# The last image's convolution: one channel tile's taps on ScalarE and GpSimd, the other two tiles' sums in PSUM

## The chip, the cores and the metric

The kernel runs on one core of a Trainium2 chip. A core has five engines with queues of their own: TensorE (PE, matrix products, with its weight loads listed apart as PEld), VectorE (DVE), ScalarE (ACT), GpSimd (POOL) and SyncE (SP, which starts transfers). SBUF is the working memory; TensorE writes its products to PSUM, which is divided into banks of 512 float32 values for each of the 128 partitions. The metric is the device time of one execution in microseconds, lower is better.

## The reference

The input x has 8 images of 384 channels and 64x64 pixels, all float32. Two layers follow each other, each adding its result to its input:

```python
# layer 0: window attention (8x8 windows, half of the heads on a shifted grid)
x = x + attention(group_norm(x), ...)
# layer 1: what this change is about
t = einsum('bchw,oc->bohw', group_norm(x), w_in)
t = irfft2(rfft2(blocks_of_8x8(t)) * fft_filter)          # per channel
t = depthwise_conv_3x3(t, w_dw)                            # 9 taps per channel
x1, x2 = t[:, :192], t[:, 192:]
x = x + einsum('bchw,oc->bohw', gelu(x1) * x2, w_out)
```

The change touches the depthwise convolution, the product of gelu(x1) and x2, and the output product with w_out.

## The kernel before

An image is worked on in 8 strips of 8 rows (512 pixels). The 384 channels are three tiles of 128 partitions, so an operation on one tile of a strip is 128x512. The attention of one image and the second layer of the image before it run interleaved; when the attention of the last image (number 7) is over, only second layers are left: the last strips of image 6's and all of image 7's.

The second layer of a strip goes through these pieces:

- `normal_x1` (L652, ScalarE) normalises the strip into xn. `mix` (four products pt on TensorE, L662 copies to SBUF on ScalarE) applies w_in. `transform` (products pf, multiplied by the filter on VectorE at L679) goes to the frequency domain, and `back` (products pz) returns from it.
- `inner` and `borders` (L707, L716, L717, ScalarE) bring pz to SBUF as z, a tile of 10 rows of 66 pixels, and exchange one border row with the strip above.
- `conv` makes the nine taps. Tap 4 is a scaled copy on ScalarE (L752), the other eight are one operation on VectorE each (L758): z shifted, times the channel's weight in `dw_sb`, plus the sum so far in zz. Taps 6 to 8 need the lower border row, so they wait for the strip below.
- For the last image and for strip 7 of image 6, the table `on_pe` gives TensorE the first five taps of tile 1: `conv_taps` multiplies z by diagonal matrices (made by `tap_matrices`) and adds up in a PSUM tile pc, from which VectorE's taps 5 to 8 go on. For the very last strip TensorE makes five taps of tile 2 and all nine of tile 1.
- `gate` applies Gelu (L771, L772, ScalarE) and multiplies (L773, L774, L775, VectorE). Hidden channels are laid out so that tiles 0 and 1 hold x1 and x2 of 128 channels, and tile 2 holds both halves of the other 64.
- `finish` is the output product pw on TensorE, its addition to the strip's input on VectorE (L797, L799) and the transfer to HBM (L800).

Each call `at(place, piece, ...)` gives a piece a place on a common axis on which a strip takes two units. The pieces are issued in the order of these places. Matmuls keep that order on TensorE. On the other engines a scheduler may reorder what has no explicit order between it, and it then inserts the waits. PSUM is used in two ways: four single banks (`psum`) that are taken in turn, and two pairs of banks (`psum2`).

`FETCHES` and the counting before the last loop belong to empty instructions that are put among the matmuls of images before the last; the pieces that the change touches lie behind them.

The lines that the tables below and the text refer to are those of this listing:

Of the kernel before, what the change touches and what calls it, by code (L numbers as in the profile page):

```python
# [7 lines left out]
F32 = mybir.dt.float32  # L8
AF = mybir.ActivationFunctionType
# [3 lines left out]
P = 128  # L13
# [24 lines left out]
def block_kernel(ctx: ExitStack, tc: tile.TileContext, out, x, consts, fsel, wqk, wv, bqk, bv,  # L38
# [21 lines left out]
    def matmul(*args, **kw):  # L60
        tc.keep_in_program_order(nc.tensor.matmul(*args, **kw))  # L61
        fetched["count"] += 4

        n = min(fetched["empty"], fetched["share"])
        for _ in range(n):
            tc.keep_in_program_order(nc.tensor.nop(hint="empty"))
        fetched["empty"] -= n
        fetched["count"] += n
# [8 lines left out]
    def row512(tag, bufs, name):  # L77
        return sb.tile([P, ST], F32, tag=tag, bufs=bufs, name=name)
# [222 lines left out]
    def at(place, piece, *args):  # L301
        plan.append((place, len(plan), piece, args))
# [1 line left out]
    xs, ys, y2s, qks, vs, os_, ots, x1s, zs = ({} for _ in range(9))  # L304

    z_bufs = [cp.tile([P, WS + 2, SW + 2], F32, name=f"z{i}") for i in range(7)]
    zs["count"] = 0
    for z in z_bufs:
        nc.gpsimd.memset(z[:, :, 0:1], 0.0)
        nc.gpsimd.memset(z[:, :, SW + 1:SW + 2], 0.0)  # L310
# [408 lines left out]


    TAPS = (4, 0, 1, 2, 3, 5, 6, 7, 8)
    on_pe = {(B - 1, s): {1: 5} for s in range(NS - 1)}
    on_pe[B - 2, NS - 1] = {1: 5}
    on_pe[B - 1, NS - 1] = {2: 5, 1: 9}

    def tap_matrices():
        d = strip("y", 3, "taps").rearrange("p k (t c) -> p (k t) c", c=P)
# [6 lines left out]
    def conv_taps(b, s):  # L734
        pc = psum2(f"pc_{b}_{s}")
        for i, (m, n) in enumerate(on_pe[b, s].items()):
            zs[b, s, "zz", m] = pc[:, i]
            for j in range(n):
                dy, dx = TAPS[j] // 3, TAPS[j] % 3
                matmul(pc[:, i], zs["taps"][m][:, j], zs[b, s, m][:, dy:dy + 8, dx:dx + SW],  # L740
                       start=(j == 0), stop=(j == n - 1))

    def conv(b, s, m, tap):

        z = zs[b, s, m]
        n = on_pe.get((b, s), {}).get(m, 0)
        if tap < max(n, 1):
            return
        if tap == max(n, 1):
            zz = row512("zz", 5, f"zz_{b}_{s}_{m}")  # L750
            if n == 0:
                after_out(nc.scalar.activation(zz.rearrange("p (r c) -> p r c", c=SW), z[:, 1:9, 1:SW + 1],  # L752
                                               AF.Copy, scale=dw_sb[:, m, 4:5]))
                zs[b, s, "zz", m] = zz
            zs[b, s, "acc", m] = zz
        acc, old = zs[b, s, "acc", m], zs[b, s, "zz", m]
        dy, dx = TAPS[tap] // 3, TAPS[tap] % 3
        i = nc.vector.scalar_tensor_tensor(acc.rearrange("p (r c) -> p r c", c=SW),  # L758
                                           z[:, dy:dy + 8, dx:dx + SW], dw_sb[:, m, TAPS[tap]:TAPS[tap] + 1],
                                           old.rearrange("p (r c) -> p r c", c=SW), ALU.mult, ALU.add)  # L760

        if b < B - 1 and m and tap == 1:
            tc.keep_in_program_order(i)
        if b < B - 1:
            after_softmax(i)
        zs[b, s, "zz", m] = acc

    def gate(b, s):
        zz = {m: zs[b, s, "zz", m] for m in range(KC)}
        g1 = row512("g1", 2, f"g1_{b}_{s}")  # L770
        nc.scalar.activation(zz[0], zz[0], AF.Gelu)  # L771
        nc.scalar.activation(g1[64:P], zz[2][0:64], AF.Gelu)  # L772
        nc.vector.tensor_tensor(g1[0:64], g1[64:P], zz[2][64:P], ALU.mult)  # L773
        nc.vector.tensor_tensor(g1[64:P], g1[64:P], zz[2][64:P], ALU.mult)  # L774
        nc.vector.tensor_tensor(zz[0], zz[0], zz[1], ALU.mult)  # L775
        zs[b, s, "g"] = zz[0], g1

    def finish(b, s):


        g0, g1 = zs[b, s, "g"]
        t = xs[b, s, "finish"]

        pw = [psum(f"pw_{b}_{s}_{m}") for m in range(2)]
        pw2 = psum2(f"pw2_{b}_{s}")
        full, lo, hi = slice(0, ST), slice(0, 256), slice(256, ST)
        pw = [(pw[0], 0, full), (pw[1], 1, full), (pw2[:, 0, lo], 2, lo), (pw2[:, 1, lo], 2, hi)]

        for i, half, r in ((0, 0, 0), (1, 1, 1), (0, 1, 0), (1, 0, 1), (2, 0, 0), (3, 1, 1), (2, 1, 0), (3, 0, 1)):
            p, m, tok = pw[i]  # L790
            rows, cols = slice(r * 64, (r + 1) * 64), slice(half * 64, (half + 1) * 64)
            matmul(p[cols], wo_sb[rows, 1, m * P + half * 64:m * P + half * 64 + 64], g1[rows, tok],
                   start=True, stop=False)
        for p, m, tok in pw:
            matmul(p, wo_sb[:, 0, m * P:(m + 1) * P], g0[:, tok], start=False, stop=True)
        for m in range(2):
            nc.vector.tensor_tensor(t[:, m, :], pw[m][0], t[:, m, :], ALU.add)  # L797
        by_half = t[:, 2, :].rearrange("p (o n) -> p o n", o=2)
        zs["added"] = nc.vector.tensor_tensor(by_half, pw2[:, :, lo], by_half, ALU.add)  # L799
        nc.sync.dma_start(out=rows_of(out[b], s), in_=t)  # L800
# [5 lines left out]
    for b in range(B):  # L806
# [73 lines left out]
        for s in range(NS):  # L880
            u = first + 2 + 2 * s
            at(u - 0.84, load, b, s, "mix")
            at(u + 0.02, normal_x1, b, s)
            for i in range(4):
                at(u + (0.28, 0.45, 0.60, 0.78)[i], mix, b, s, i)
            for j in range(2):
                at(u + (0.995, 1.02)[j], transform, b, s, j)
            if b < B - 1:
                at(u + 1.985, small_tiles, u + 2)
            at(u + 1.99, back, b, s)  # L890
            at(u + 2.08 if b < B - 1 or s < NS - 1 else u + 1.991, borders, b, s)

            for n, m in enumerate((0, 2, 1)):
                for tap in range(1, 6):
                    at(u + (2.62, 3.10, 3.5)[n] + 0.05 * tap + (0.4 if n == 2 and tap > 3 else 0), conv, b, s, m, tap)
                for tap in range(6, 9):
                    at(u + 4.2 + 0.25 * (n * 3 + tap - 6) / 9, conv, b, s, m, tap)
            if (b, s) in on_pe:
                at(u + 2.3, conv_taps, b, s)
            at(u + 5.16, load, b, s, "finish")  # L900
            at(u + 4.5, gate, b, s)
            at(u + 6.10, finish, b, s)
# [6 lines left out]
    count, dense, empty = fetched["count"], [], [0] * len(order)  # L909
    for i, (piece, args) in enumerate(order):  # L910
        count += 4 * sum(on_pe[args].values()) if piece is conv_taps else FETCHES.get(piece.__name__, 0)
        if piece in (qk_tile, project):
# [121 lines left out]
```

## Time and profile before

| what | value |
| --- | --- |
| time, median of 3 runs | 3572.18 us (3568.28 to 3581.91) |
| profiled execution: span | 3571.7 us (the page gives no other time for it) |
| TensorE busy | 3489.3 us, 98% |
| VectorE busy | 3059.8 us, 86% |
| ScalarE busy | 2475.3 us, 69% |
| GpSimd busy | 953.0 us, 27% |
| L758, VectorE taps | 1483 + 9 operations, 744 ns in the middle |
| L752, ScalarE scaled copies | 182 operations, 719 ns |
| L380, GpSimd sums of 128x512 | 122 operations, 1282 ns in the middle, 1263 to 2361 |
| pc<-z,taps on TensorE | 108 matmul records, 47.8 us in all |

The span runs from the first instruction to the last. A busy share is an average over the whole span, so the stage that the change touches has to be looked up by itself. A float32 matmul appears as two records. In a row of instructions, "out<-in" are the program's names with the buffer numbers left out, then the shape, "x" the count, and a bracket gives the idle time before it and what ended it.

### The profile page before, as it was taken

The numbers are of one execution on the slowest core, as the hardware profiler recorded it, in microseconds if no ns is written. First come the engines' busy times: TensorE is split into PE (matmuls) and PEld (weight loads), VectorE is DVE, ScalarE is ACT, GpSimd is POOL, SyncE is SP. The second block draws the span as 40 slices with busy tenths as digits, with TensorE's granted clock in tenths as the row PEclk, the third lists the DMA queues.
The fourth block names the chain that finished last, engine by engine and source line by source line (L and its number), as shares of the span: only waits on it lengthen the run. The fifth ranks groups of instructions, "written<-read, shape, count | busy, mean of one in ns | idle before, by whom it ended". The sixth has DMA issues, their size and how long they took to land.

```text
span 3571.7 us, 93732 instructions
## 1 busy us (share of the span) xinstructions
PE 3489.3 (98%) x36598; PEld 2209.2 (62%) x36598; DVE 3059.8 (86%) x4370; ACT 2475.3 (69%) x3983; POOL 953.0 (27%) x1616
## 2 busy tenths in 40 slices
PE   7999999999999999999999999999999999999998
PEld 5666666666666666666666666666666656666554
DVE  4766689889988899888998889988899888887988
ACT  4777677768777677776777767777777768776442
POOL 5333222223222232222232223222232223221000
PEclk8999999999999999999999999999999999999999
DMA  4333333234333334333333334333334233333431
GB/s 124 115 124 111 104 113 133 101 105 158 127 121 116 114 125 158 103 112 134 126 130 124 118 106 143 133 103 134 123 120 148 100 106 122 100 104 108 156 116 72
DMA packets 177254, 427.45 MB, mean 120 GB/s; under 512 B 26784, under 2 KB 29371, under 8 KB 176840
## 3 DMA queue, kind: packets, MB, share of 16 engines
q1 hardware_dynamic: 139984, 370.54, 29.6%
q0 software_dynamic: 36416, 50.65, 5.1%
q8 instruction: 318, 5.21, 0.6%
q14 instruction: 96, 0.79, 0.1%
q10 hardware_dynamic: 440, 0.27, 0.0%
HBM read 270.21 MB, written 100.79 MB: 104 GB/s over the span
## 4 chain that ended last, share of the span: by engine, by line
PE 88%; DVE 8%; ACT 2%; DMA 1%; issue 1%; SPq 0%; ACTq 0%; DVEq 0%
PE pq L61 26%; PE pr L61 14%; PE pvv L61 13%; PE pt L61 11%; PE pw L61 6%; DVE zz L758 4%; PE pA L61 4%; PE pz L61 3%; PE pS L61 3%; PE pT L71 3%; PE pf L61 2%; PE ln L61 1%; DVE t L679 0%; DMA x_stats<-in_x_dram 0%; DVE e L535 0%
## 5 line engine op out<-in xcount | busy, mean ns | idle before, releaser
L758 DVE SCALAR_TENSOR_TENSOR zz<-z,dw_sb,zz 128x512 f32<-128x512 f32 x1483 | 1117.8, 783 | 26.2 <-ACT z L716 14.9
L61 PE MATMUL pq<-y,wqk_sb 128*128 128x512 f32 x2160 | 999.8, 600 | 0.9 <-DVE y L436 0.8
L613 POOL DMA_DIRECT2D oT<-o x960 | 480.4, 508 | 981.3 <-ACT z L716 442.4
L61 PEld LDWEIGHTS pq<-y,wqk_sb 128*128 128x128 f32 x2160 | 400.7, 190 | 459.9 <-issue 416.1
L61 PE MATMUL pt<-wi_sb,xn 128*128 128x384 f32 x1536 | 536.0, 487 | 7.6 <-ACT kcd L468 4.8
L61 PE MATMUL pr<-oT,wp_sb 128*128 128x512 f32 x1152 | 522.5, 592 | 0.0
L61 PE MATMUL pvv<-wv_sb,y 128*128 128x192 f32 x2880 | 508.5, 326 | 0.0
L61 PEld LDWEIGHTS pvv<-wv_sb,y 128*128 128x128 f32 x2880 | 470.7, 190 | 47.7 <-issue 32.7
L61 PEld LDWEIGHTS pt<-wi_sb,xn 128*128 128x128 f32 x1536 | 289.4, 190 | 234.9 <-issue 76.7
L450 POOL COPY y<-y 128x384 f32<-128x384 f32 x112 | 83.4, 744 | 1136.6 <-PE pvv L61 665.1
L61 PEld LDWEIGHTS pr<-oT,wp_sb 128*128 128x128 f32 x1152 | 218.6, 190 | 268.6 <-issue 249.9
L468 ACT ACTIVATE kcd<-pq,bqk_sb 32x512 f32<-32x512 f32 x512 | 348.4, 680 | 9.0
L468 ACT ACTIVATE qab<-pq,bq_sb,cst 96x512 f32<-96x512 f32 (+1 forms) x256 | 197.6, 772 | 199.2 <-PE pq L61 196.6
L501 ACT COPY v<-pvv 128x384 f32<-128x384 f32 x256 | 121.6, 475 | 212.6 <-PE pvv L61 211.4
L468 ACT ACTIVATE kab<-pq,bqk_sb 96x512 f32<-96x512 f32 (+1 forms) x256 | 174.1, 680 | 96.9 <-PE pq L61 92.4
L468 ACT ACTIVATE qcd<-pq,bq_sb,cst 96x512 f32<-96x512 f32 (+1 forms) x256 | 197.5, 772 | 35.9 <-PE pq L61 29.1
L662 ACT COPY t<-pt 128x384 f32<-128x384 f32 x256 | 122.5, 479 | 128.9 <-PE pt L61 124.8
L528 DVE TENSOR_TENSOR e<-pS,bias 128x512 f32<-128x512 f32 (+2 forms) x200 | 108.1, 547 | 114.6 <-PE pS L61 114.4
L380 POOL TENSOR_TENSOR sq<-sq 128x512 f32<-128x512 f32 x122 | 200.9, 1647 | 5.8
L535 DVE TENSOR_TENSOR e<-e,mx 128x1024 f32<-128x1024 f32 x128 | 198.7, 1553 | 4.1
L61 PE MATMUL pw<-zz,wo_sb 128*128 128x512 f32 (+1 forms) x512 | 183.4, 501 | 0.0
L545 DVE TENSOR_REDUCE rc<-e 128x16 f32<-128x1024 f32 x128 | 155.0, 1211 | 29.6 <-ACT e L540 29.6
(151 smaller groups left out, 5185.7 us busy)
## 6 DMA issues: line engine op xcount, KB each, us to landing
x_add<-in_x_dram SPq DMA_DIRECT2D x64, 768.0 KB, 9.6
x1d<-x_add SPq DMA_DIRECT2D x64, 768.0 KB, 3.7
x_mix<-x1d SPq DMA_DIRECT2D x64, 768.0 KB, 5.4
x_finish<-x1d SPq DMA_DIRECT2D x64, 768.0 KB, 7.2
out_dram<-x_finish SPq DMA_DIRECT2D x64, 768.0 KB, 4.2
x_norm<-in_x_dram SPq DMA_DIRECT2D x61, 768.0 KB, 7.4
x_stats<-in_x_dram SPq DMA_DIRECT2D x56, 768.0 KB, 7.6
oT<-o POOLq DMA_DIRECT2D x192, 96.0 KB, 3.8
```

Source lines behind the costliest of these rows:

```text
L61: tc.keep_in_program_order(nc.tensor.matmul(*args, **kw))
L71: tc.keep_in_program_order(nc.tensor.transpose(*args, **kw))
L380: nc.gpsimd.tensor_tensor(sq[:, 0, :], sq[:, 0, :], sq[:, k, :], ALU.add)
L450: nc.gpsimd.tensor_copy(dst[:, :, :, :, 0:4], src[:, :, :, :, 4:8])
L468: return nc.scalar.activation(dst[to:to + n], pq[of:of + n], AF.Identity, bias=bias[of:of + n], scale=scale)
L501: nc.scalar.copy(v[:, 384 * g:384 * (g + 1)], pvv[:, 0:384])
L528: nc.vector.tensor_tensor(e5[:, odd, :, a:z, :], pS[:, odd, :, a:z, :], bias_t[br, kind, odd].unsqueeze(2).to_broadcast([P, 2, z - a, 64]) ...
L535: zs["soft"] = nc.vector.tensor_tensor(e, e, mx.unsqueeze(2).to_broadcast([P, 2 * NS, 64]), ALU.subtract)
L545: nc.vector.tensor_reduce(rc, e, AX.X, ALU.add)
L613: nc.gpsimd.dma_start(out=oT[to % P:to % P + z - a, to // P, rows], in_=o[row + a:row + z, h // 2, of:of + n])
L662: nc.scalar.copy(t1, pt[:, 0:C])
L758: i = nc.vector.scalar_tensor_tensor(acc.rearrange("p (r c) -> p r c", c=SW), z[:, dy:dy + 8, dx:dx + SW], dw_sb[:, m, TAPS[tap]:TAPS[tap] ...
```

## The change

For strip 7 of image 6 and strips 0 to 6 of image 7 (the list `on_pool`), three things change.

1. Tile 1 leaves TensorE and VectorE. ScalarE makes all nine taps as scaled copies, two to a buffer (three buffers, taken over from the attention, whose tags are "o", "e" and "eT"), and GpSimd adds them up in SBUF (`pool_taps`).
2. Tiles 0 and 2 keep their sum in a pair of PSUM banks from tap 4 to the gate; VectorE's taps read and write it in place. Gelu of tile 0 writes its result to SBUF.
3. The product of tile 0 and tile 1 in `gate` moves from VectorE to GpSimd. As a PSUM pair is in use for the sums, `finish` takes three single banks for its output in place of two banks and a pair, and its third tile is computed as one 512-wide piece.

The last strip of image 7 keeps its taps on TensorE and VectorE.

```diff
-    on_pe = {(B - 1, s): {1: 5} for s in range(NS - 1)}
-    on_pe[B - 2, NS - 1] = {1: 5}
-    on_pe[B - 1, NS - 1] = {2: 5, 1: 9}
+    on_pe = {(B - 1, NS - 1): {2: 5, 1: 9}}
+    on_pool = [(B - 2, NS - 1)] + [(B - 1, s) for s in range(NS - 1)]
...
+    def pool_taps(b, s, taps):
+
+        z = zs[b, s, 1]
+        for j in range(0, len(taps), 2):
+            tag = ("o", "e", "eT")[zs["pairs"] % 3]
+            zs["pairs"] += 1
+            pair = sb.tile([P, 2, ST], F32, tag=tag, bufs=1, name=f"tap_{b}_{s}_{taps[j]}")
+            for i, tap in enumerate(taps[j:j + 2]):
+                dy, dx = TAPS[tap] // 3, TAPS[tap] % 3
+                nc.scalar.activation(pair[:, i].rearrange("p (r c) -> p r c", c=SW), z[:, dy:dy + 8, dx:dx + SW],
+                                     AF.Copy, scale=dw_sb[:, 1, TAPS[tap]:TAPS[tap] + 1])
+            if tap == 1:
+                zz = zs[b, s, "zz", 1] = row512("qk", 5, f"zz_{b}_{s}_1")
+                nc.gpsimd.tensor_tensor(zz, pair[:, 0], pair[:, 1], ALU.add)
+            else:
+                zz = zs[b, s, "zz", 1]
+                for i in range(len(taps[j:j + 2])):
+                    nc.gpsimd.tensor_tensor(zz, zz, pair[:, i], ALU.add)
...
     def conv(b, s, m, tap):
 
+        if m == 1 and (b, s) in on_pool:
+            return
...
         if tap == max(n, 1):
-            zz = row512("zz", 5, f"zz_{b}_{s}_{m}")
+            if (b, s) in on_pool:
+                if m == 0:
+                    zs[b, s, "in psum"] = psum2(f"acc_{b}_{s}")
+                zz = zs[b, s, "in psum"][:, m // 2]
+            else:
+                zz = row512("zz", 5, f"zz_{b}_{s}_{m}")
...
     def gate(b, s):
...
-        nc.scalar.activation(zz[0], zz[0], AF.Gelu)
+        if (b, s) in on_pool:
+            whole = row512("zz", 5, f"zz_{b}_{s}_0")
+            nc.scalar.activation(whole, zz[0], AF.Gelu)
+            zz[0] = whole
+        else:
+            nc.scalar.activation(zz[0], zz[0], AF.Gelu)
...
-        nc.vector.tensor_tensor(zz[0], zz[0], zz[1], ALU.mult)
+        (nc.gpsimd if (b, s) in on_pool else nc.vector).tensor_tensor(zz[0], zz[0], zz[1], ALU.mult)
...
     def finish(b, s):
...
-        pw = [psum(f"pw_{b}_{s}_{m}") for m in range(2)]
-        pw2 = psum2(f"pw2_{b}_{s}")
+        pw = [psum(f"pw_{b}_{s}_{m}") for m in range(3 if (b, s) in on_pool else 2)]
+        if (b, s) in on_pool:
+            pw = [(p, m, full) for m, p in enumerate(pw)]
+        else:
+            pw2 = psum2(f"pw2_{b}_{s}")
+            pw = [(pw[0], 0, full), (pw[1], 1, full), (pw2[:, 0, lo], 2, lo), (pw2[:, 1, lo], 2, hi)]
...
+            if i < len(pw) and not (len(pw) == 3 and i == 2):
...
+        if len(pw) == 3:
+            matmul(pw[2][0], wo_sb[0:64, 1, 2 * P:3 * P], g1[0:64], start=True, stop=False)
...
+        if len(pw) == 3:
+            nc.vector.tensor_tensor(t[:, 2, :], pw[2][0], t[:, 2, :], ALU.add)
+            nc.sync.dma_start(out=rows_of(out[b], s), in_=t)
+            return
...
+            if (b, s) in on_pool:
+                for place, taps in ((2.45, (0, 1)), (2.8, (2, 3)), (3.15, (4, 5)), (4.15, (6, 7)), (4.3, (8,))):
+                    at(u + place, pool_taps, b, s, taps)
```

More of the change, by code (lines that the diff above doesn't have):

```diff
@@ L306, in block_kernel @@
     z_bufs = [cp.tile([P, WS + 2, SW + 2], F32, name=f"z{i}") for i in range(7)]
-    zs["count"] = 0
+    zs["count"] = zs["pairs"] = 0
     for z in z_bufs:
@@ L782, in finish @@
         t = xs[b, s, "finish"]
-        pw = [psum(f"pw_{b}_{s}_{m}") for m in range(2)]
-        pw2 = psum2(f"pw2_{b}_{s}")
         full, lo, hi = slice(0, ST), slice(0, 256), slice(256, ST)
-        pw = [(pw[0], 0, full), (pw[1], 1, full), (pw2[:, 0, lo], 2, lo), (pw2[:, 1, lo], 2, hi)]
-        for i, half, r in ((0, 0, 0), (1, 1, 1), (0, 1, 0), (1, 0, 1), (2, 0, 0), (3, 1, 1), (2, 1, 0), (3, 0, 1)):
[L790 to L793, printed above, removed]
+        pw = [psum(f"pw_{b}_{s}_{m}") for m in range(3 if (b, s) in on_pool else 2)]
[4 more added lines that the diff above has]
+            pw = [(pw[0], 0, full), (pw[1], 1, full), (pw2[:, 0, lo], 2, lo), (pw2[:, 1, lo], 2, hi)]
+        for i, half, r in ((0, 0, 0), (1, 1, 1), (0, 1, 0), (1, 0, 1), (2, 0, 0), (3, 1, 1), (2, 1, 0), (3, 0, 1)):
+            if i < len(pw) and not (len(pw) == 3 and i == 2):
+                p, m, tok = pw[i]
+                rows, cols = slice(r * 64, (r + 1) * 64), slice(half * 64, (half + 1) * 64)
+                matmul(p[cols], wo_sb[rows, 1, m * P + half * 64:m * P + half * 64 + 64], g1[rows, tok],
+                       start=True, stop=False)
+        if len(pw) == 3:
+            matmul(pw[2][0], wo_sb[0:64, 1, 2 * P:3 * P], g1[0:64], start=True, stop=False)
         for p, m, tok in pw:
@@ L911, in block_kernel @@
         count += 4 * sum(on_pe[args].values()) if piece is conv_taps else FETCHES.get(piece.__name__, 0)
+        if piece is finish and args in on_pool:
+            count -= 16
         if piece in (qk_tile, project):
```

## Prediction

> **What bounds the kernel now.** I read the forty slices of the page first. The change concerns the last image's convolution, so I need the place where GpSimd has run out of work:
>
> ```profile
> DVE  4766689889988899888998889988899888887988
> ACT  4777677768777677776777767777777768776442
> POOL 5333222223222232222232223222232223221000
> ```
>
> From about 3360 us on GpSimd (POOL) is free and ScalarE (ACT) falls to 4 tenths, while VectorE (DVE) stays at 8 to 9. Next I cut that end into stretches, each from one strip's transform products (L679) to the next strip's. From 3404.4 to 3532.7 there are six equal ones of 21.4 us; one of them, and a short stretch just before them:
>
> ```profile
> core 0: us, PE busy (x) PEld busy (x) DVE busy (x) ACT busy (x) POOL busy (x), PEclk, DMA share, GB/s
> 3468.50:3489.90 21.40, 19.93 (x186) 11.64 (x186) 19.15 (x31) 9.21 (x21) 0.00 (x0) 1.00 0.31 111
> 3384.00:3387.50 3.50, 3.50 (x98) 3.38 (x98) 3.39 (x6) 1.70 (x4) 0.00 (x0) 0.54 0.43 173
> ```
>
> TensorE 19.93 and VectorE 19.15 of 21.40 are too close to say which bounds. The chain of waits says it:
>
> ```profile
> 3461.36 7.17 DVE zz L758 x11
> 3468.53 0.03 issue
> 3468.56 1.95 DVE t L679 x4
> 3470.51 0.04 issue
> 3470.56 0.77 PE pz L61 x32
> 3471.32 1.17 ACT z L707 x2
> ```
>
> It is VectorE everywhere, except for a bridge of some 2 us (inverse transform on TensorE, copy and border copy on ScalarE) in which VectorE waits. The timelines of VectorE and TensorE show the wait and the slack:
>
> ```profile
> 3472.63 4.06 DVE L758 SCALAR_TENSOR_TENSOR zz<-z,dw_sb,zz 128x512 f32<-128x512 f32 x6 [2.13 <-ACT z L716]
> 3478.07 4.46 PE L61 MATMUL pc<-z,taps 128*128 128x512 f32 x10
> 3488.27 1.53 PE L61 MATMUL pf<-t,cst 64*64 64x192 f32 x32
> 3491.03 0.69 PE L61 MATMUL pz<-cst,t 64*64 64x64 f32 x32 [1.23 <-DVE t L679]
> ```
>
> pf ends at 3489.80; its first half is there by about 3489.05 and VectorE takes it up at 3489.95. So TensorE has about 0.9 us of slack a strip: whoever shortens VectorE alone gains 0.9 and no more. The change shortens both.
>
> **The change part by part.**
>
> *VectorE, removed.* Four taps of tile 1 (it had taps 5 to 8; the sum of taps 0 to 4 came in pc) and the product L775 for each of eight strips. The chain has 11 taps in 7.17 us, 0.652 each; start to start in the timeline they stand 0.663 apart, which I take. L775 starts 0.70 before the next. 4 x 0.663 + 0.70 = 3.35 us a strip. In its order: one tap in the onset (before 3382.7), 3.35 in each of seven stretches, and 2.69 (three taps, one product) after 3532.7.
>
> *VectorE, in another memory.* The 16 remaining taps read and write PSUM. For reading the trace has rows by form, between 3400 and the end:
>
> ```profile
> L758 DVE SCALAR_TENSOR_TENSOR zz<-z,dw_sb,zz 128x512 f32<-128x512 f32 x137 | 94.8, 745 | 15.6 <-ACT z L716 14.9
> ...
> L758 DVE SCALAR_TENSOR_TENSOR zz<-z,dw_sb,pc 128x512 f32<-128x512 f32 x8 | 5.9, 741 | 0.0
> ```
>
> So the PSUM operand costs nothing: 741 against 745 ns. [...] I take the row, which measures this very instruction. [...]
>
> *TensorE, removed.* Five matmuls of 128x512, the ten records pc above: 4.3 us a strip (4.46 with overlap). The output product loses four 64-row pieces and its two halves of tile 2 for one 64-row product and one full one: 16 records of g in 1.5 us and 8 of zz in 2.85 become about 1.8 and 2.6; even. TensorE's work goes from 19.93 to 15.6.
>
> *GpSimd, added.* Eight sums and one product of 128x512 a strip. The nearest row is the sum L380, of the same shape and in SBUF: 1263 ns at the least, 1282 in the middle, 2361 at most. 9 x 1.28 = 11.5 us, 12.4 with 0.1 between two. The product waits for Gelu of tile 0, with the next strip's sums queued behind it; TensorE's output product waits for it in place of L775. The plan puts that output product 1.6 of a strip's two units after the gate, some 14 us, and GpSimd has 18 - 12.4 = 5.6 us to spare: 0. Why up to 2361 shows in two places:
>
> ```profile
> 1039.61 3.50 POOL L380 TENSOR_TENSOR sq<-sq 128x512 f32<-128x512 f32 x2
> 1039.90 2.08 DVE L535 TENSOR_TENSOR e<-e,mx 128x1024 f32<-128x1024 f32 x1
> 1041.90 2.42 DVE L758 SCALAR_TENSOR_TENSOR zz<-z,dw_sb,zz 128x512 f32<-128x512 f32 x2
> ...
> 2551.95 0.68 DVE L799 TENSOR_TENSOR x_finish<-pw,x_finish 128x512 f32<-128x512 f32 x1
> 2552.28 2.62 POOL L380 TENSOR_TENSOR sq<-sq 128x512 f32<-128x512 f32 x2
> ```
>
> With two SBUF operands on VectorE the engines take turns: 2.08 for the 1.22 us that L535 takes alone in the chain at 3317.7, two taps 2.42 for the 1.41 at 3494.0, GpSimd's second sum 2.15. Beside x_finish<-pw (one operand in PSUM) nothing is longer. In the changed strips every VectorE operation has its second operand in PSUM: taps, g (zz[2] is in PSUM), L679 (pf), x_finish (pw). So there is no turn-taking there. It remains where neighbours still sum in SBUF: strip 6 of image 6, some of whose taps and whose gate run from 3360.5 to 3376, just when strip 7's five first sums want GpSimd. Each meeting costs VectorE about 1.0; I take four, +4.0 (0 to 5). At the end image 7's strip 7 sums tile 0 in SBUF, but GpSimd's last four operations should be over by then: 0 (up to 4).
>
> *ScalarE, added.* Nine scaled copies a strip; L752 is the same operation, 0.72 alone and 0.60 start to start. 9 x 0.60 = 5.4 on 9.21: 14.6 us. It hides beside VectorE as long as nothing blocks it, but it is in order: Gelu, z and border copies stand behind the copies. I allow half a copy in their way, 0.3 us, in eight strips: +2.4. Gelu reading PSUM and the two first taps written to PSUM: L707 reads PSUM at 655 ns, Gelu reads SBUF at 631; 0.
>
> *Queues and space.* No DMA is added or moved; SP's order stays. The sums' PSUM pair lives from tap 4 to the gate, about one strip, with two such pairs: no wait. The output product now takes three of the four single banks, so the mix products wait for x_finish one bank sooner. pw is done about 4.3 us after pz, x_finish about 5 after the border copy, and one mix product (1.94) still fits before: 0.
>
> **The sum.** A stretch becomes 21.40 - 3.35 = 18.05 for VectorE, its wait of 2.13 kept. TensorE would need 21.40 - 0.9 - 4.3 = 16.2, ScalarE 14.6, GpSimd 12.4: VectorE still bounds, and what is late next is TensorE. Onset: +4.0 - 0.66 = +3.3. Seven stretches: -23.4. End: -2.7 (there TensorE's pc, 12.18 us for the last strip, is ready at 3552.5, when the chain needed it at 3553.9; most of the gain stays). ScalarE's queue: +2.4. Together -20.4. The profiled execution has a span of 3571.7 us; the page has no other time of it, and the median of the three runs, 3572.18, is 0.5 away, so I put the difference on the median: 3552.
>
> **The rivals.**
> *A, as summed* (0.58): 3543 to 3558.
> *B, the bridge is filled* (0.12). With pf earlier against the taps, the order may put L679 before the last taps of tile 2, and these fill the 2.13 us. Then TensorE's cycle, 15.6 + 1.5 of waiting for L679, sets 17.1: another 0.95 x 7 = 6.7, 3544; without the onset's cost 3540. For: pf now has a third less in front of it. Against: today all eleven taps stand before L679.
> *C, the gain is eaten by half* (0.13). One mechanism is the clock. In the row of 3384.0 TensorE had 0.54 of its clock after a wait of 2.51 us, and pz took 4.02 in place of 2.30. [...] That speaks against taking work off TensorE, whose idle time grows to about 2.4 us a strip. [...] The rows of the six stretches stand at 1.00 with 1.5 us idle, in pieces up to 1.23, and matmuls fill the rest of each window: I keep 1.00. [...]
> *D, slower* (0.17): ScalarE stands behind GpSimd. Three buffers carry the pairs; a copy of a fourth pair waits for two sums (2.6 us), and with it all that is queued on ScalarE, z and Gelu among it, on which VectorE waits. GpSimd's product in turn waits for Gelu. The point is 21.4 - 14.6 = 6.8 us of blocking a strip. With four waits of 2.6 the stretch is 25 us, 8 x 3.6 = 29 longer, 3601. Against: GpSimd works 12.4 of 18 us and is ahead by the next pair.
> *No effect:* would need VectorE not to bound; the chain excludes that.
>
> **How the numbers follow.** This kernel's measurement can tell about 0.5%, 18 us, from no change: 3554 to 3590. Of A two thirds lie below 3554 (0.39), of B all: faster 0.51. The rest of A (0.19) and C (0.13): same 0.32. D: slower 0.17. The range 3540 to 3575 takes A, B, C and leaves out D and the edge of B; A's own is 3543 to 3558.
>
> **What would show it.** Stretches between two L679 of about 18 us (right), 17 (B), above 20 (C, D). Taps zz in PSUM at 740 to 750 ns and 0.66 apart; above 800 the memory step is wrong. GpSimd's sums at 1.28 from the second strip on, longer beside strip 6 of image 6. ScalarE near 14.6 us a stretch and no wait of its own for GpSimd; if tap copies wait for GpSimd, D. TensorE's clock at 1.00. A wait of VectorE other than for L716 would put my 2.13 wrong.

## The result and the profile after

The changed kernel takes 3565.77 us (median of 12 runs, 3555.03 to 3572.54) against 3570.10 us (12 runs, 3566.16 to 3581.91): ratio 0.9984, 95% interval 0.9974 to 0.9993. That is 4.3 us less, not the 20 that were forecast, and less than the 0.5% up to which the prediction speaks of no change. The profiled execution took 3566.98 us, span 3565.2.

The two programs are the same up to the last image's attention. Up to the L679 of strip 7 of image 6 the changed one is 2.8 us later (3358.99 against 3356.22 us), with the same instructions, so this is drift between executions (over the twelve traces of this document that L679 starts between 3345.8 and 3359.2 us). What the change does lies in the tail behind that L679, and I measure every kernel there:

| us | before | changed | difference | forecast |
| --- | --- | --- | --- | --- |
| onset: L679 of strip 7, image 6, to L679 of strip 0, image 7 | 26.49 | 30.05 | +3.6 | +3.3 |
| the seven stretches to the L679 of strip 7 | 150.05 | 137.34 | -12.7 | -23.4 |
| from there to the end | 38.89 | 38.74 | -0.15 | -2.7 |
| allowance for ScalarE's queue | | | in the rows above | +2.4 |
| tail | 215.42 | 206.13 | -9.3 | -20.4 |

Of the 9.3 us of the two traces the medians show 4.3, interval 2.5 to 9.3. So the tail of this one profile sits at the good edge, and the figures below are about where the time went, not about its last microsecond.

In the listing of the changed kernel VectorE's taps are L783 (L758 before), the products with Gelu L803 and L804 (L773, L774), the product of tile 0 and tile 1 L805 (L775), the two Gelu L798 and L802, the first tap of tile 0 and 2 L777 (L752), the addition of pw L833 and L835. New are L751 (ScalarE's tap copies) and L759 (GpSimd's sums). The experiments shift these by some lines; the names stay.

The forty slices of the changed kernel's page, three of its rows:

```profile
DVE  5766589889988899988998989988899888987987
ACT  4777677768777687776777767777777767776564
POOL 5333222223232233222323223223223222222244
```

In the last three slices ScalarE has gone from 4, 4 and 2 tenths to 5, 6 and 4, and GpSimd from nothing to 2, 4 and 4: the work moved as planned. Two of its stretches (the columns are those of the table of stretches shown in the prediction: TensorE, weight loads, VectorE, ScalarE, GpSimd, TensorE's clock, DMA):

```profile
3408.60:3427.60 19.00, 16.59 (x168) 9.46 (x168) 17.83 (x28) 15.22 (x31) 11.39 (x9) 1.00 0.38 126
3467.30:3487.30 20.00, 18.21 (x168) 10.64 (x168) 16.53 (x25) 14.31 (x30) 11.39 (x9) 0.91 0.34 120
```

ScalarE has the 14.3 us that were forecast (14.6), GpSimd 11.4 (12.4). But no engine is full any more: in 20.00 us VectorE works 16.53. And TensorE's clock is at 0.91 in four of the seven stretches, 0.86 in the first and 1.00 in only two. The clock itself is 1.00 or 0.50 in these traces, never between. A stretch at 0.91 holds one piece of 3.41 us at 0.50; here is that piece, and the 3.41 us before it:

```profile
3466.36:3469.77 3.41, 1.51 (x48) 0.95 (x40) 3.34 (x7) 1.43 (x3) 0.92 (x1) 1.00 0.26 56
3469.77:3473.18 3.41, 3.29 (x70) 2.64 (x64) 1.02 (x3) 1.99 (x5) 0.00 (x0) 0.50 0.44 180
```

It falls on pz, just behind the wait for L679. In the 3.41 us ahead of it TensorE worked 1.51 us. At the same place of a stretch before the change (3489.61 to 3493.02) it worked 1.95 us, and the clock stayed at 1.00. The chain of waits of the changed kernel tells what a stretch hangs on now:

```profile
3474.02 1.25 ACT tap L751 x2
3475.40 0.52 POOL zz L759
...
3476.76 1.28 POOL zz L759
3478.07 1.33 ACT tap L751 x2
3479.42 1.33 ACT tap L751 x2
...
3482.07 0.60 ACT g L802
3482.70 0.70 DVE g L803
```

Before, this chain was VectorE's taps with a bridge of 2 us. Now it goes from z through ScalarE's copies, GpSimd's sums, ScalarE again and Gelu, and only then back to VectorE. The timelines of ScalarE and of VectorE in the same stretch show both ends of it:

```profile
3478.07 2.69 ACT L751 ACTIVATE tap<-z,dw_sb 128x512 f32<-128x512 f32 x4 [0.97 <-POOL zz L759]
...
3482.07 0.59 ACT L802 ACTIVATE g<-acc 64x512 f32<-64x512 f32 x1
```

```profile
3472.28 3.69 DVE L783 SCALAR_TENSOR_TENSOR acc<-z,dw_sb,acc 128x512 f32<-128x512 f32 x5 [2.35 <-ACT z L716]
...
3482.70 0.69 DVE L803 TENSOR_TENSOR g<-g,acc 64x512 f32<-64x512 f32 x1 [0.76 <-ACT g L802]
...
3484.14 3.13 DVE L783 SCALAR_TENSOR_TENSOR acc<-z,dw_sb,acc 128x512 f32<-128x512 f32 x4
```

The fourth pair's copies wait 0.97 us for a buffer that GpSimd still reads. Behind all nine copies (5.9 us) stand Gelu and, at 3483.06, the first tap of tile 2. So VectorE first waits 0.76 us for Gelu, and then has nothing but tile 2's taps left, each of which needs the one before: four in 3.13 us, 0.79 apart. Mixed with tile 0's they stand 0.66 apart.

### The profile page after: what moved, and what is told of

Its sections match the earlier page's. It is cut to its first block, busy times and chain, and to the rows that moved or that the text cites. A ratio compares the mean times of both kernels' runs of the same rounds, so it can differ in the third digit from the quotient of the medians.

```text
span 3565.2 us, 93610 instructions
## 1 busy us (share of the span) xinstructions
PE 3472.5 (97%) x36454; PEld 2203.4 (62%) x36454; DVE 3048.4 (86%) x4330; ACT 2519.4 (71%) x4055; POOL 1047.6 (29%) x1688
## 4 chain that ended last, share of the span: by engine, by line
PE 88%; DVE 6%; ACT 3%; DMA 1%; issue 1%; POOL 1%; SPq 0%; ACTq 0%; POOLq 0%; DVEq 0%
PE pq L61 26%; PE pr L61 14%; PE pvv L61 13%; PE pt L61 11%; PE pw L61 6%; PE pA L61 4%; PE pz L61 4%; PE pS L61 3%; PE pT L71 3%; PE pf L61 2%; DVE zz L783 2%; PE ln L61 1%; DVE acc L783 1%; ACT tap L751 1%; DVE e L535 1%
## 5 line engine op out<-in xcount | busy, mean ns | idle before, releaser
L783 DVE SCALAR_TENSOR_TENSOR zz<-z,dw_sb,zz 128x512 f32<-128x512 f32 x1331 | 1021.0, 793 | 10.9
L61 PE MATMUL pw<-zz,wo_sb 128*128 128x512 f32 x496 | 182.2, 510 | 0.0
L623 DVE SCALAR_TENSOR_TENSOR x_add<-pr,vec,x_add 128x512 f32<-128x512 f32 x192 | 142.9, 744 | 36.4 <-PE pr L61 35.6
```

The lines of the kernel that those rows point to most:

```text
L623: after_softmax(nc.vector.scalar_tensor_tensor(t[:, m, :], pr, bp_sb[:, m:m + 1], t[:, m, :], ALU.add, ALU.add))
```

## The experiments

All are the changed kernel with one edit, except where more are named. The ratio is to executions of the kernel before that ran beside the version; their median was 3573.64 (the first four below), 3570.89 (the next four) and 3573.03 us (the last two). A median is over 4 to 20 executions. Onset, stretches, end and "tail" are those of the table above and come from one trace each (tail: 215.42 before, 206.13 changed), so small differences between versions are not to be leaned on.

| edit | median us | ratio to before (95%) | onset | the seven stretches, mean | end | tail |
| --- | --- | --- | --- | --- | --- | --- |
| none (changed kernel) | 3565.77 | 0.9984 (0.9974 to 0.9993) | 30.05 | 19.62 | 38.74 | 206.1 |
| pf twice | 3568.58 | 0.9986 (0.9978 to 0.9994) | 30.83 | 19.89 | 37.98 | 208.1 |
| fourth pair buffer | 3559.26 | 0.9964 (0.9953 to 0.9976) | 30.03 | 18.97 | 37.83 | 200.6 |
| ScalarE's order | 3554.64 | 0.9958 (0.9943 to 0.9974) | 23.57 | 18.89 | 39.49 | 195.3 |
| VectorE's order | 3553.87 | 0.9951 (0.9936 to 0.9966) | 30.02 | 17.93 | 38.30 | 193.9 |
| image 6's strip as before | 3567.46 | 0.9988 (0.9978 to 0.9997) | 26.50 | 20.54 | 40.90 | 211.2 |
| sums in SBUF | 3612.48 | 1.0119 (1.0103 to 1.0135) | 30.59 | 25.66 | 38.34 | 248.5 |
| both orders | 3550.10 | 0.9946 (0.9925 to 0.9966) | 23.03 | 18.56 | 39.96 | 192.9 |
| both orders, last strip too | 3559.63 | 0.9967 (0.9955 to 0.9980) | 23.27 | 18.56 | 47.13 | 200.3 |
| VectorE's order, ScalarE's at the onset | 3551.49 | 0.9941 (0.9926 to 0.9955) | 23.04 | 18.44 | 38.31 | 190.4 |
| the same, fourth pair buffer | 3547.51 | 0.9928 (0.9914 to 0.9943) | 23.04 | 18.17 | 39.88 | 190.1 |

**Is it the clock, or ScalarE's queue?** Two theories stood after the result: that the stretches are long because TensorE's clock falls (rival C of the prediction), or because Gelu and tile 2's first tap stand behind the copies. The first edit keeps TensorE busier, by issuing the 16 products pf of every strip of image 7 twice, into the same place:

```diff
                     matmul(pf_[p][cols, i * 192:(i + 1) * 192], fwd[rows, rows],
                            t1[rows, h * 192:(h + 1) * 192], start=True, stop=True)
+                    if b == B - 1:
+                        tc.keep_in_program_order(nc.tensor.matmul(
+                            pf_[p][cols, i * 192:(i + 1) * 192], fwd[rows, rows],
+                            t1[rows, h * 192:(h + 1) * 192], start=True, stop=True))
```

> The changed kernel, but in image 7 each transform product pf is made twice (same values over themselves), which adds 1.5 us of dense TensorE work a strip just before the wait for L679. In the changed kernel this also joins the four L679 again, which there stand as two and two with a tap between. Clock theory (TensorE's halved clock, 0.91 in a stretch, lengthens pz from 2.3 to 4 us and with it the bridge): granted clock 1.00 in all stretches, pz 2.3 us, stretches from 19.8 to about 19.0, end stretch from 38.8 to about 37; in all 5 us shorter. Queue theory (ScalarE's order sets the stretch, TensorE is off the path): clock 1.00 as well, but stretches stay at 19.8 to 20. TensorE-bound theory: stretches 1.5 us longer, 21.3.

The clock was 1.00 in five of the seven stretches instead of two, and four of those five took 19.6 us, the fifth 20.2. The time did not move (0.9986 against 0.9984). The test is not clean: the added products cost TensorE some 1.5 us a strip themselves, and the edit also joined the four L679, which in the changed kernel mostly stand two and two with a tap between (1.95 us in place of 2.61). But a full clock alone does not bring 18 us.

The second edit takes away ScalarE's wait for GpSimd, with a fourth buffer for the pairs of copies:

```diff
-            tag = ("o", "e", "eT")[zs["pairs"] % 3]
+            tag = ("o", "e", "eT", "sq")[zs["pairs"] % 4]
...
-            pair = sb.tile([P, 2, ST], F32, tag=tag, bufs=1, name=f"tap_{b}_{s}_{taps[j]}")
+            if tag == "sq":
+                pair = strip("sq", 1, f"tap_{b}_{s}_{taps[j]}")[:, 0:2]
+            else:
+                pair = sb.tile([P, 2, ST], F32, tag=tag, bufs=1, name=f"tap_{b}_{s}_{taps[j]}")
```

> The changed kernel with a fourth buffer for the pairs of scaled copies, so that ScalarE need not wait for GpSimd's sums. Theory that ScalarE stands behind GpSimd (0.97 us a strip in the trace): the wait is gone, Gelu comes 1 us sooner, stretches from 19.8 to about 18.9. Theory that the nine copies ahead of Gelu and of tile 2's first tap do it: the wait is gone from ScalarE but VectorE's chain of tile 2 still starts late, gain at most 1 us a stretch and only as far as the wait itself; clock theory: nothing changes.

The wait of the copies is gone, VectorE's for Gelu falls from 4.2 us in the seven stretches together to 0.2, and the stretches at full clock are 18.5 to 18.7. Those at 0.91 take 19.2 and 19.3. Yet all nine copies still stand in front of Gelu. One stretch, first ScalarE and then VectorE, which starts the product with Gelu without a wait:

```profile
3447.76 5.62 ACT L754 ACTIVATE tap<-z,dw_sb 128x512 f32<-128x512 f32 x9
```

```profile
3455.88 0.69 DVE L806 TENSOR_TENSOR g<-g,acc 64x512 f32<-64x512 f32 x1
```

So it was the 0.97 us behind GpSimd, inside the block of copies, that made VectorE wait for Gelu; the block without it fits. The buffer was worth 5.5 us of tail (0.0020 of the ratio), and the lower clock some 0.6 us a stretch where it occurs.

The third edit leaves every operation as it is and changes only ScalarE's order: tile 2's first tap directly behind the previous strip's Gelu, and the second and third pair of copies behind it.

```diff
+                if tap in (2, 3, 4, 5):
+                    behind(a, zs[b, s, "tile 2"], mybir.DependencyClass.NoSync, "tile 2 first")
...
+                if m == 2 and (b, s) in on_pool:
+                    zs[b, s, "tile 2"] = i
+                    if "gelu" in zs:
+                        behind(i, zs["gelu"], mybir.DependencyClass.NoSync, "Gelu first")
...
-                for place, taps in ((2.45, (0, 1)), (2.8, (2, 3)), (3.15, (4, 5)), (4.15, (6, 7)), (4.3, (8,))):
+                for place, taps in ((2.45, (0, 1)), (3.2, (2, 3)), (3.3, (4, 5)), (4.15, (6, 7)), (4.3, (8,))):
```

> The changed kernel with an order on ScalarE: tile 2's first tap comes after the Gelu of the strip before, and the copies of the pairs (2,3) and (4,5) come after tile 2's first tap. Queue theory (Gelu and tile 2's first tap wait behind nine copies, so VectorE waits 0.8 us for Gelu and then runs tile 2's taps alone, 0.79 apart): no wait of VectorE for Gelu, Gelu some 3.5 us earlier in the stretch, stretches from 19.8 to about 18.5, in all 8 us shorter. Clock theory: VectorE's wait for Gelu goes, but the stretch stays above 19.3 since the bridge stays long. If GpSimd's sums, now later, come on the path: the output product waits for the product on GpSimd, stretch 20 or more.

This removes the same wait in another way, for nearly the same mean stretch (18.89 against 18.97). VectorE's wait for Gelu is gone in all steady stretches, and the chain is VectorE and the bridge once more. Two stretches of this kernel, with the columns as above:

```profile
3420.14:3439.52 19.38, 18.08 (x162) 10.28 (x165) 16.44 (x25) 14.19 (x29) 11.22 (x10) 0.91 0.33 123
3458.18:3476.84 18.66, 17.34 (x175) 9.69 (x171) 16.34 (x25) 14.32 (x30) 11.43 (x10) 1.00 0.35 128
```

The one stretch at 0.91 is 0.7 us longer than those at 1.00, 0.63 of it a wait of VectorE for the output product. What is left over the forecast's 18.05 is 0.6 us: tile 2's last taps still run alone, 0.79 apart (its VectorE works 16.34 us, where 19.15 - 3.35 = 15.8 were forecast). The onset fell by 6.5 us too, which I had not foreseen; it is taken up below.

The fourth edit changes only VectorE's order: taps 1 to 5 of tile 2 go behind the next strip's L679, into the bridge.

```diff
-            nc.vector.tensor_tensor(t2[:, p], pf_[p][:, 0:C].rearrange("p (i c) -> p i c", i=2),
+            zs["filtered"] = nc.vector.tensor_tensor(t2[:, p], pf_[p][:, 0:C].rearrange("p (i c) -> p i c", i=2),
...
+        if m == 2 and tap < 6 and (b, s) in on_pool:
+            behind(i, zs["filtered"], mybir.DependencyClass.NoSync, "filter first")
```

> The changed kernel with an order on VectorE: the taps 1 to 5 of tile 2 come after the next strip's L679, so that they lie in the bridge (inverse transform, copies) in which VectorE waits 2.35 us. Bridge theory: no wait of VectorE for the border copies left, Gelu and tile 2's start are no longer ahead of L679, TensorE's cycle of 16.6 us and 0.6 us of handover sets the stretch: 17 to 17.5, in all 14 us shorter, clock 1.00 since TensorE waits less. Queue theory alone: ScalarE's run of 14.3 us plus its wait for GpSimd and for pz still sets it, stretch 18.5 to 19.5. If the clock stays at 0.91: 18 to 18.5.

Stretches of 17.87 us at a clock of 1.00, though VectorE still waits 1.61 us for Gelu and ScalarE still 0.96 us for GpSimd in each: these waits no longer decide. Which engine does, is seen below in the last version.

**What the onset costs.** The forecast put +3.3 us on four meetings of GpSimd's sums and VectorE operations with two operands in SBUF. The changed kernel's timelines of VectorE and of GpSimd at the onset:

```profile
3367.34 3.36 DVE L783 SCALAR_TENSOR_TENSOR zz<-z,dw_sb,zz 128x512 f32<-128x512 f32 x2
...
3372.49 7.81 DVE L783 SCALAR_TENSOR_TENSOR zz<-z,dw_sb,zz 128x512 f32<-128x512 f32 x7
...
3381.64 1.65 DVE L803 TENSOR_TENSOR g<-g,zz 64x512 f32<-64x512 f32 x1
3383.33 1.65 DVE L805 TENSOR_TENSOR zz<-zz,zz 128x512 f32<-128x512 f32 x1
```

```profile
3381.18 4.92 POOL L759 TENSOR_TENSOR zz<-zz,tap 128x512 f32<-128x512 f32 x3 [2.76 <-ACT tap L751]
```

The products take 1.65 us, 0.69 where GpSimd rests, and GpSimd's three sums 4.92, where three in the steady part take 3.98: they take turns. Taken one by one, eight operations of VectorE in the onset are stretched to 1.65 to 1.79 us, five taps (in the first two rows) and three products: 7.9 us in all, for the four meetings and 4.0 us of the forecast. Before the change none is. Strip 7 of image 6 was given back to TensorE and VectorE:

```diff
-    on_pe = {(B - 1, NS - 1): {2: 5, 1: 9}}
-    on_pool = [(B - 2, NS - 1)] + [(B - 1, s) for s in range(NS - 1)]
+    on_pe = {(B - 2, NS - 1): {1: 5}, (B - 1, NS - 1): {2: 5, 1: 9}}
+    on_pool = [(B - 1, s) for s in range(NS - 1)]
```

> The changed kernel with strip 7 of image 6 taken out of the new form: its tile 1 is again made by TensorE (five taps) and VectorE (four), its sums lie in SBUF. Turn-taking theory (in the changed kernel GpSimd's five first sums meet the SBUF taps and the gate of strip 6 on VectorE, 1.0 us each; the onset from the filter of strip 7 of image 6 to the filter of image 7's strip 0 grew from 26.5 to 30.1 us): the onset is back at 26.5 and the L758 and gate rows in it at 0.75 and 0.69. The next stretch loses what the strip had gained, 3.4 us on VectorE at the most, so it lies between 19.5 and 21.7. The six stretches stay at 19.0 to 20.0. Rival (the onset grew because ScalarE's table loads and copies delay Gelu): the onset stays above 28.

The onset is 26.50 us, that of the kernel before (26.49). So the onset's cost comes from this strip's part of the change. The whole did not get faster, because the later stretches fell out unevenly: in the second VectorE waits 2.74 us for Gelu, and the clock differs. Two of them:

```profile
3448.31:3470.34 22.03, 20.84 (x164) 11.51 (x168) 16.73 (x25) 13.25 (x27) 11.37 (x9) 0.77 0.32 108
3470.34:3489.67 19.33, 17.21 (x180) 9.59 (x172) 16.34 (x25) 16.04 (x32) 11.40 (x9) 1.00 0.33 120
```

One strip's work is 2.7 us longer at a granted clock of 0.77, 2.54 of it VectorE's wait for the output product. The 0.77 is 10.24 us at 0.50 in succession (from 3450.00), three pieces where the changed kernel's stretches have one. Why it did not come back sooner is not settled.

With ScalarE's order of the third edit the onset is 23.57 us, less than before the change: tile 1's copies come later, GpSimd starts its sums after the gate of strip 6, and the products are back at 0.69. The meeting was a matter of order: one tap is stretched in place of eight operations.

**What PSUM is worth.** Tiles 0 and 2 sum in SBUF as before, everything else as changed:

```diff
-                if m == 0:
-                    zs[b, s, "in psum"] = psum2(f"acc_{b}_{s}")
-                zz = zs[b, s, "in psum"][:, m // 2]
+                zz = row512("zz", 5, f"zz_{b}_{s}_{m}")
```

> The changed kernel with the sums of tiles 0 and 2 in SBUF again; all else as changed (tile 1 on ScalarE and GpSimd, product on GpSimd, three output banks). Turn-taking theory: each of GpSimd's nine operations a strip meets a tap with two SBUF operands, so VectorE pays up to 9 x 1.0 us and GpSimd 9 x 0.65: taps at 1.7 us beside a sum, sums up to 2.1, stretches from 19.8 to between 24 and 28 us, the kernel 30 to 60 us slower than changed. If PSUM operands were what cost in the changed kernel (dependent taps 0.79 apart): stretches fall to 19 or less. If neither matters: 19.8.

42 us slower than before the change, with stretches of 25.9. Its groups of VectorE's taps and GpSimd's sums from 3411 us on, and under them the same two of the changed kernel from 3408 to 3527:

```profile
L781 DVE SCALAR_TENSOR_TENSOR zz<-z,dw_sb,zz 128x512 f32<-128x512 f32 x97 | 101.2, 1112 | 15.5 <-ACT z L716 15.3
L759 POOL TENSOR_TENSOR zz<-zz,tap 128x512 f32<-128x512 f32 x42 | 67.4, 1604 | 71.8 <-ACT tap L751 69.5
```

```profile
L783 DVE SCALAR_TENSOR_TENSOR acc<-z,dw_sb,acc 128x512 f32<-128x512 f32 x99 | 71.5, 752 | 12.9 <-ACT z L716 11.2
L759 POOL TENSOR_TENSOR zz<-zz,tap 128x512 f32<-128x512 f32 x42 | 53.5, 1274 | 52.7 <-ACT tap L751 49.9
```

With the sum in SBUF a tap takes 1112 ns and a sum 1604, with it in PSUM 752 and 1274. Without part 2 of the change, part 1 would have been a loss: some 6 us in each stretch hang on where the sum lies, which a tap both reads and writes. (This kernel's clock was at 0.83 in these stretches, so TensorE may have a share in the 6 us; but VectorE's busy time alone grew from 16.5 to 23.2 us a stretch.)

**Can the gain be had?** Both orders together, the diffs of the third and the fourth edit:

> Both orders together: on ScalarE Gelu and tile 2's first tap before the pairs (2,3) and (4,5); on VectorE taps 1 to 5 of tile 2 after the next strip's L679. Each alone left one wait: the ScalarE order alone the 2.0 us for the border copies (stretch 18.66), the VectorE order alone 1.6 us for Gelu (17.87). If these waits are separate, both go, and a stretch is VectorE's 16.0 us of work or TensorE's 16.5 and a handover: 16.6 to 17.2, with the onset at 23.6 as in the ScalarE order alone; 3543 to 3549 in all. If they share a cause (ScalarE is full at 14.4 us with its waits for pz): 17.6 to 17.9 as with the VectorE order alone.

Onset 23.0, as with ScalarE's order, but stretches of 18.59, longer than the 17.87 of VectorE's order alone. ScalarE's timeline around the L679 at 3442.96:

```profile
3442.46 2.56 ACT L751 ACTIVATE tap<-z,dw_sb 128x512 f32<-128x512 f32 x4
3444.92 2.21 ACT L652 ACTIVATE xn<-x_mix,sh,gs_b 128x512 f32<-128x512 f32 x3
3447.04 1.16 ACT L707 ACTIVATE z<-pz 128x512 f32<-128x512 f32 x2
```

Now four copies stand in front of xn and of z, which starts 4.08 us after the L679; with VectorE's order alone it starts 2.75 us after it. VectorE, through with its five taps of tile 2, waits 0.88 us for the first tap of tile 0 of the new strip, which needs z. The two orders get in each other's way in the steady part. Then the last strip was given the new form as well, in place of its taps on TensorE:

```diff
-    on_pe = {(B - 1, NS - 1): {2: 5, 1: 9}}
-    on_pool = [(B - 2, NS - 1)] + [(B - 1, s) for s in range(NS - 1)]
+    on_pe = {}
+    on_pool = [(B - 2, NS - 1)] + [(B - 1, s) for s in range(NS)]
...
-        if b == B - 1:
-            at(first + 2, tap_matrices)
```

> As the one with both orders, and the very last strip in the new form too: no taps on TensorE any more, the matrices for them not made. If the end is bound by TensorE (12.18 us of taps in a row before the last two output products, VectorE waits 0.8 to 1.3 us for them): the end stretch falls from 38.8 by 3 to 5 us, GpSimd's nine operations (11.5 us after the border copies) being the next bound. If it is bound by VectorE's tail: it gains 1 at most, since VectorE then makes all 16 taps of the last strip. If by GpSimd: it is longer than 38.8, and the last output product waits for GpSimd's product.

The end is 7.2 us longer than with both orders alone (47.13 against 39.96). In its chain of waits an output product stands for 10.44 us; its 16 records take 4.75 us in a steady stretch of the last version below, at a clock of 1.00:

```profile
3526.01 10.44 PE pw L61 x16
```

The granted clock from 3525.2 to 3533.2 is 0.50, after TensorE had stood idle for 8.46 us; with both orders alone it is 1.00 from 3498.7 to 3526.7. The next output product takes 9.17 us, where the last one takes 5.96 with both orders alone. The taps on TensorE in the last strip do not only do work: in the kernel that has them the clock stayed at 1.00 up to 3526.7, in the one without them it was at 0.50 for 8.0 us, and its output products took the longer times above.

Last, each order only where it helped: VectorE's in all changed strips, ScalarE's only for strip 7 of image 6, without and with the fourth pair buffer. Beside the diffs above, against the third edit:

```diff
-                if tap in (2, 3, 4, 5):
+                if tap in (2, 3, 4, 5) and b < B - 1:
...
-                    if "gelu" in zs:
+                    if "gelu" in zs and b < B - 1:
...
-                for place, taps in ((2.45, (0, 1)), (3.2, (2, 3)), (3.3, (4, 5)), (4.15, (6, 7)), (4.3, (8,))):
+                for place, taps in ((2.45, (0, 1)), (3.2 if b < B - 1 else 2.8, (2, 3)),
+                                    (3.3 if b < B - 1 else 3.15, (4, 5)), (4.15, (6, 7)), (4.3, (8,))):
```

> Both orders, each only where it has helped: VectorE's (tile 2's taps 1 to 5 behind the next strip's L679) in all changed strips, ScalarE's (tile 2's first tap behind Gelu, two pairs behind that) only for strip 7 of image 6. Queue theory, with the two effects independent: onset 23 us as with ScalarE's order alone (30 in the changed kernel), then stretches of 17.9 as with VectorE's order alone, end 38 to 39; from the L679 of strip 7 of image 6 to the end about 187 us (206 changed, 215 before), a median some 18 us under the changed kernel's, ratio to the kernel before 0.993 to 0.994. Rival, the short onset only moves the wait (image 7's first stretch takes back what the onset gives): onset 23 and a first stretch of over 22, tail about 193. Rival, clock: with less work in the onset TensorE's clock falls in the steady stretches, 18.6 to 18.9 each, tail about 193.

> The same with a fourth pair buffer. With VectorE's order ScalarE still stood 0.96 us a strip behind GpSimd and VectorE 1.61 us behind Gelu. Queue theory: the copies no longer wait for GpSimd, Gelu comes about 0.9 us earlier, and the stretch falls from 17.9 to about 17.0; tail about 181. Rival, TensorE's cycle (predicted 16.2) or another ScalarE wait takes the place: stretches of 17.4 to 17.9, tail 184 to 187. Rival, clock: TensorE idles longer in a shorter stretch and the granted clock falls below 1.00; 18 or more.

The onset came as expected (23.04), and the steady stretches are 17.87 in both. But the first two stretches of image 7 took part of it back, 21.00 and 18.67 us without the fourth buffer, 19.50 and 18.29 with it; in the first of these, without the buffer, VectorE waits 3.2 us for tile 0's first tap, behind copies that wait 1.5 and 1.4 us for GpSimd, which now does image 6's sums and image 7's in one stretch. So the two gains are not independent, and of the tail of 187 us that I expected 190.4 came. The fourth buffer was expected to bring the steady stretch to 17.0, and did nothing there. This version's chain says why:

```profile
3469.26 1.95 DVE t L679 x4
3471.21 0.04 issue
3471.25 1.61 PE pz L61 x64
3472.86 4.75 PE pw L61 x16
3477.61 7.74 PE pt L61 x24
3485.36 1.78 PE pf L61 x32
```

TensorE's cycle, 4.75 + 7.74 + 1.78 + 1.61 with L679 in it, 1.95 + 0.04, is 17.87 us. That is rival B's bound, forecast at 17.1. With the fourth buffer this has the lowest median of all: 3547.51 us, ratio to the kernel before 0.9928 (0.9914 to 0.9943), 18 us under the changed kernel. Its interval overlaps those of both orders and of the version without the buffer, whose tail is 190.4 against 190.1, so which of the three is fastest is not shown.

## Why the prediction failed

The forecast was 3552 us and the measured median 3565.8. The range held it (3540 to 3575), the case "same" (0.32) came and not the likeliest. By the steps of the sum:

- *Right: the work.* ScalarE 14.3 us a stretch (14.6 forecast), GpSimd's sums 1.27 us each and the engine 11.4 (12.4). VectorE's taps in PSUM took 752 ns, where the rows that I went by had 741 and 745. Those rows show PSUM read; that writing it costs nothing was put into the sum without a run that shows it. The changed kernel's taps, which read and write it, took 7 ns more than those in SBUF, some 0.1 us over the 16 taps of a strip.
- *Right in its cause, by luck in its number: the onset*, +3.6 for +3.3. The turn-taking is there, and the onset is 26.50 us without this strip's part. But eight operations met a sum and not four, +7.9, more than the 0 to 5 that I had allowed; and seven taps fewer lie in the onset (23 in place of 30, some of them only moved on) and not one, some -4.6. The two errors cancel. That an order can avoid the meetings was not seen.
- *Wrong: the stretches*, -12.7 for -23.4. The step that failed is ScalarE's: "It hides beside VectorE as long as nothing blocks it", with "half a copy in their way, 0.3 us", and the reason given against rival D, that GpSimd "is ahead by the next pair". I had named the mechanism in the same lines, Gelu and z behind the copies, and priced it by half of one copy, as if the copies lay spread out. They come as a block of nine, 5.9 us, with a wait of 0.97 for GpSimd in the middle, and what VectorE needs next is at its back. The fourth buffer shows that the wait in the middle is the part that reaches VectorE: without it, and with the nine still in front, VectorE waits 0.2 us for Gelu in the seven stretches and not 4.2. A stretch should have been 18.05. Over seven stretches 137.34 - 7 x 18.05 = 11.0 us are too much. By the runs these fall apart roughly like this: tile 2's taps alone at 0.79 and not 0.66, 0.6 a stretch (what ScalarE's order left at full clock), some 4; the wait for Gelu, 4.2 in all; the clock, 0.6 to 0.8 in each of four, some 2.5. They add up to 10.7. This is an estimate: the parts overlap, and each comes from another kernel. Half of rival D (ScalarE behind GpSimd) had come true, at 0.97 us a strip and not four times 2.6, and in place of a loss it ate a gain.
- *Wrong: the clock kept at 1.00.* It was 0.91 in four stretches. The row of 3384.0 (0.54, behind a wait of 2.51 us) spoke against the change, and I set it aside. The 1.7 us by which pz was longer there (4.02 in place of 2.30) would be too much for every strip, at 0.91 it is 0.6 to 0.8 (18.66 against 19.38 us in one kernel); my 0 was too low. The row I argued from, 1.00 with 1.5 us idle, held for a stretch in which TensorE was otherwise full for 19.9 of 21.4 us. What brings the halving on, the traces do not show: TensorE had worked 1.51 us in the 3.41 before the piece shown above, so it had not been idle there. What share of work keeps the clock up, no run here isolates: VectorE's order had 1.00 with 16.5 us of work in 17.9.
- *Wrong: the end*, -0.15 for -2.7. I had written beside the number that pc was ready 1.4 us before it was needed, and still counted 2.7: TensorE alone capped the gain at 1.4. Then pc itself came later. The timeline of TensorE at the end:

```profile
3528.58 2.87 PE L61 MATMUL pz<-cst,t 64*64 64x64 f32 x62 [0.24 <-DVE t L679]
...
3536.03 12.18 PE L61 MATMUL pc<-z,taps 128*128 128x512 f32 x28
```

  This part of pz, at half clock, took 1.61 us before, and the output product ahead of pc had grown by 0.6 us. So pc, no shorter, ended 21.8 us after the L679, 19.8 before, and VectorE waited 1.33 us for it. The last output product gave much of this back: its clock was 0.57 before (3560.8 to 3564.8) and is 1.00 now, and VectorE waits 3.09 us for it in place of 4.65. The result near zero is a sum of terms that cancel.
- *TensorE's relief was over-counted.* I called the output product even, and it grew from 4.30 to 4.92 us a stretch: the ten records with 64 rows take 2.15 us, and the six full ones 2.84, as long as the eight before. This was hidden in the stretches of the changed kernel and is 0.6 of the 0.8 us by which rival B's 17.1 missed 17.87. (B's total, 3552 less 6.7, is 3545 and not 3544.)

The work left the engines as forecast. With VectorE's order changed, and not one operation, the seven stretches are 24.5 us shorter than before, where the sum had 23.4; but TensorE's cycle of 17.87 us sets them then, not VectorE's 18.05. That ScalarE's order has a tail 20.1 us shorter, where the sum had 20.4, is chance: its stretches are only 17.8 us shorter, and its onset is 2.9 shorter where 3.3 more was forecast. What failed is the assumption that an engine with free time also has it at the right moment.

## What to carry to other kernels

When work moves to an engine with free time, write down the order of its queue in one period and count what stands in front of each result that the bounding engine waits for. Count the waits inside that block too: here the block alone fitted, and 0.97 us of waiting in it did not. Before counting a gain, work out the next engine's whole cycle, its waits for others included; here it was TensorE's, 17.87 us. And take work off TensorE only after asking what its clock does then, in that stage and in the one behind it.

## What the hardware showed that was not expected

- Four VectorE taps that each need the one before take 3.13 us (0.79 apart), mixed with taps of another tile 0.66 apart: 0.13 us for each dependent pair, some 0.6 us a strip. It is not PSUM that does this. Before the change, with the sum in SBUF, tile 0's taps alone in the last strip stand as far apart:

```profile
3546.87 6.32 DVE L758 SCALAR_TENSOR_TENSOR zz<-z,dw_sb,zz 128x512 f32<-128x512 f32 x8
```

- In these traces the clock of TensorE is halved for 3.41 us at a time, or several times that (in the changed kernel 6.83 us from 3370.79 on, 3.41 us from 3469.77 on). In one kernel a strip took 19.33 us at a granted clock of 1.00 and 22.03 at 0.77, with the same work, and with VectorE's order alone the halving stayed away from all the steady stretches.
- Where the sum lies decides whether VectorE and GpSimd work side by side: a tap and a sum of GpSimd take 752 and 1274 ns with VectorE's sum in PSUM, 1112 and 1604 with it in SBUF.
